# A scoring kernel's first two chunks: splits moved ahead of copies, two blocks taken part by part, one store halved

## The chip, the cores and the metric

The kernel runs on one core of one Trainium2 chip. The metric is the device time of one execution in microseconds, lower is better. The engines are named as in the profile: PE is TensorE (matmuls, PEld its weight loads), DVE is VectorE, ACT is ScalarE, POOL is GpSimd, and SP is the queue of SyncE that issues most DMAs.

## What is computed

1024 sequences of 50 item numbers, a table of 100001 rows of 128 floats, and one output of 1024 x 100001 floats (409.6 MB):

```
emb = emb_table.at[0].set(0.0)
e = emb[seq]                                  # 1024 x 50 x 128
prefix = jnp.cumsum(e, axis=1)
uF = prefix / jnp.minimum(t_idx, lengths)     # running mean
y = (uF - mean) * rsqrt(var + BN_EPS) * gamma + beta      # over the batch
v = v + (x - v) / 2; spike = v >= 1; v = v - spike        # 50 steps, one neuron per feature
uF_out = spikes.mean(axis=0)                  # 1024 x 128
scores = uF_out @ emb.T                       # 1024 x 100001
```

## The kernel before

It has two phases. The first (to about 510 us) gathers rows for the 50 steps and counts the spikes of every sequence and feature. The counts end as eight weight tiles of 128 x 128, one for each *block* `n` of 128 sequences: `countA` for block 0, `countB` for blocks 1 to 4, `countC` for blocks 5 to 7. The change is in the second phase, which multiplies them with the whole table and stores 409.6 MB.

**Parts and chunks.** The table is cut into 98 *parts* `q` of 1024 rows (`HALF`). A chunk `c` holds as many parts as `WIDTHS` says: four chunks of 2, four of 3, thirteen of 6. Parts, blocks and chunks are counted from 0 here; the words "third store" and "parts three and four" of the change's title count from one and mean block 2 of chunk 0 and parts 2 and 3.

**Split of a part** (`prepare`, lines 148 to 153). PE turns the part by eight transposes into a PSUM tile `pt` (L136); ACT casts it to a high half `hi` (L152); DVE subtracts `hi` from it, which leaves `lo` (L153). Such a pair takes one place from the list `free`. A product of one block and one part (`product`, L160) is four matmuls: `hi` and `lo` for each of two banks of 512 columns.

**Blocks of a chunk** (loop from line 499). For each block, for each part of the chunk: four matmuls into a PSUM tile `po`, then one copy with a factor 1/50 into the output tile `o`, on DVE (L512) or ACT (L514) in turns of a counter `turn`. The `ps` ring of four PSUM buffers holds both `po` and `pt` tiles in the order in which the code asks for them. After a block's parts one DMA on SP stores it (`store`, L169). In chunk 0, block 0 is done before the loop, and block 1 is stored in two halves. Output tiles of chunks 0 to 3 come from four buffers `o0` to `o3`, so a block's first copy waits until the store of four blocks earlier has landed: block 7 of chunk 0 for block 3, block 0 of chunk 1 for block 4 of chunk 0, and so on.

**When the next split comes** (`ready`, L486). In chunks 0 to 3 the places for pairs are few. Chunk 0 has none over until its own parts are done with, so parts 2 and 3 are split in block 7 of chunk 0: after the copy of part 0, `free.append(split.pop(q))` gives its place to part 2 and `ready()` splits that; after the copy of part 1 the same for part 3. Part 4 is split after block 2 of chunk 1.

The schedule is written by hand: each engine runs its instructions in the order in which the code issues them, so a copy that waits for a landing holds up whatever stands behind it on its engine.

Of the kernel before, what the change touches and what calls it, by code (L numbers as in the profile page):

```python
# [12 lines left out]
F32 = mybir.dt.float32  # L13
# [7 lines left out]
P = 128  # L21
BN_EPS = 1e-5
V_TH = 1.0
HALF = 1024
KQ = HALF // P
BANK = 512
# [13 lines left out]
def rec_kernel(  # L40
# [9 lines left out]
    nc = tc.nc  # L50
    B, T = seq.shape
    N, D = table.shape
    NB = B // P
# [29 lines left out]
    split = {}  # L83

    free = []
# [4 lines left out]
    def size(q):  # L90
        return min(HALF, N - q * HALF)
# [4 lines left out]
    def group(g):  # L96
        at = g if g < AHEAD else AHEAD - 2 + g % 2
        r = rowp.tile([P, GROUP, HALF], F32, tag=f"rows{at}", name=f"rows_{g}")
        for k in range(GROUP):
            rows[g * GROUP + SHIFT + k if g else k + ASIDE * (k >= TWICE)] = r[:, k, :]  # L100
        return r

    def fetch(r, k, q, n):

        engine = nc.sync if q < held else nc.scalar
        n = min(n, parts - q)
        whole = n - (size(q + n - 1) < HALF)
        if whole:
            engine.dma_start(
                out=r[:, k : k + whole, :],  # L110
                in_=table[q * HALF : (q + whole) * HALF, :].rearrange("(q p k) d -> p q (k d)", p=P, k=KQ),
            )
        if whole < n:
            full, rest = divmod(size(parts - 1), KQ)
            c1 = (parts - 1) * HALF
            r = r[:, k + whole, :]
            if rest:
                at = full - full % 32
                nc.vector.memset(r[at : at + 32, :], 0.0)
                engine.dma_start(  # L120
                    out=r[full : full + 1, : rest * D],
                    in_=table[c1 + full * KQ : N, :].rearrange("(o k) d -> o (k d)", o=1),
                )
            if full:
                engine.dma_start(
                    out=r[:full, :],
                    in_=table[c1 : c1 + full * KQ, :].rearrange("(p k) d -> p (k d)", k=KQ),
                )
# [19 lines left out]
    def prepare(q, pt):  # L148
        turned(q, pt)
        split[q] = hi, lo = free.pop(0)  # L150
        vp, vh, vl = views(q, pt, hi, lo)
        nc.scalar.copy(vh, vp)  # L152
        nc.vector.tensor_tensor(vl, vp, vh.bitcast(F32), ALU.subtract)  # L153
# [3 lines left out]
    def product(po, q, n, k0, kw):  # L157
        kw += kw % 2
        for j, part in enumerate(split[q]):
            nc.tensor.matmul(  # L160
                po[:, :kw],
                lhsT=counts[n],
                rhs=part[:, k0 : k0 + kw],
                start=j == 0,
                stop=j == 1,
            )

    def store(n, c0, o):
        nc.sync.dma_start(out=outs[n, :, c0 : c0 + o.shape[1]], in_=o)  # L169


    with ExitStack() as ph:
# [144 lines left out]
        for t in range(T):  # L317
# [42 lines left out]
            q = sp.tile([P, 1], F32, tag="q", name=f"q_{t}")  # L360
# [20 lines left out]
            if not last:  # L381
# [16 lines left out]
                if t in (T - 8, T - 6):  # L398
                    q = (t - T + 8) // 2
# [49 lines left out]
    psum = ctx.enter_context(  # L449
        tc.tile_pool(name="psum", bufs=4, space=bass.MemoryType.PSUM, reuse_waits="tile")  # L450
    )
    opening = ExitStack()
    turn = 1
    blocks = 0
    q0 = 0
# [4 lines left out]
    def places(at):  # L460
        t = rowp.tile([P, GROUP, HALF], F32R, tag=f"rows{at}", name=f"pairs_{at}")
        free.extend((t[:, k, :], t[:, k + 1, :]) for k in range(0, GROUP, 2))

    for c, W in enumerate(WIDTHS):

        if c in (0, NARROW, MIDDLE):
            opening.close()
            if c == NARROW:
                assert third in free
                free.remove(third)  # L470
                beside.close()
            where = opening if c < MIDDLE else ctx
            op = where.enter_context(tc.tile_pool(name="o", bufs=1, reuse_waits="tile"))
            if c == 0:
                turns = [(op, f"o{k}", 2) for k in range(4)]
            elif c == NARROW:
                turns = [(op, f"o{k}", 3) for k in (2, 0, 1)]
            else:
                fourth = op.tile([P, 4, HALF], F32R, tag="pairs", name="pairs")
                free.extend((fourth[:, k, :], fourth[:, k + 1, :]) for k in (0, 2))  # L480
                turns = [(rowp, "rows2", 6), (op, "o", 6), (rowp, "rows3", 6)]
            blocks = 0
        q1 = q0 + W
        q2 = q1 + (WIDTHS[c + 1] if c + 1 < len(WIDTHS) else 0)

        def ready():  # L486
            nonlocal to_split, third
            if to_split < q2 + FURTHER.get(c, 0) and free:
                prepare(to_split, psum.tile([P, HALF], F32, tag="ps", name=f"pt_{to_split}"))
                to_split += 1  # L490

                if to_split == SHIFT:
                    t = asidep.tile([P, ASIDE, HALF], F32R, tag="aside", name="third")
                    third = (t[:, 0, :], t[:, 1, :])
                    free.append(third)
                if to_split in (GROUP + SHIFT, 2 * GROUP + SHIFT):
                    places(to_split // GROUP - 1)

        for n in range(NB):
            if c == 0 and n == 0:  # L500
                continue
            pool, tag, most = turns[blocks % len(turns)]
            blocks += 1
            o = pool.tile([P, most * HALF], F32, tag=tag, name=f"o_{c}_{n}")
            for q in range(q0, q1):
                h0 = (q - q0) * HALF
                hw = size(q)
                po = psum.tile([P, HALF], F32, tag="ps", name=f"po_{n}_{q}")
                for k0 in range(0, hw, BANK):
                    product(po[:, k0 : k0 + BANK], q, n, k0, min(BANK, hw - k0))  # L510
                if turn % 2 == 0:
                    nc.vector.tensor_scalar_mul(o[:, h0 : h0 + hw], po[:, :hw], 1.0 / T)  # L512
                else:
                    nc.scalar.mul(o[:, h0 : h0 + hw], po[:, :hw], 1.0 / T)  # L514
                turn += 1
                if c == 0 and n == 1:
                    store(n, q * HALF, o[:, h0 : h0 + hw])
                if n == NB - 1:
                    free.append(split.pop(q))
                    ready()  # L520
            if c or n > 1:
                store(n, q0 * HALF, o[:, : min(N, q1 * HALF) - q0 * HALF])
            if {0: 4, MIDDLE: 0}.get(c, 2) <= n < NB - 1:
                ready()

            if n in (1, 4) and c >= MIDDLE and to_fetch < parts:
                g, k = divmod(to_fetch - SHIFT, GROUP)
                if k or to_split >= (g - 1) * GROUP + SHIFT:
                    if k == 0:
                        r = group(g)  # L530
                    fetch(r, k, to_fetch, GROUP // 2)
                    to_fetch += GROUP // 2
        assert to_split >= q2
        q0 = q1
# [19 lines left out]
```

## Time and profile before

| what | value |
|---|---|
| time, median of 4 runs | 1574.34 us (1573.22 to 1574.96) |
| the profiled execution | 1573.87 us, span 1572.0 us |
| PE busy, share of the span | 1128.1 us, 72% |
| DVE busy | 949.5 us, 60% |
| ACT busy | 672.9 us, 43% |
| POOL busy | 380.5 us, 24% |
| DMA | 488.12 MB, mean 311 GB/s |
| mean granted PE clock | 0.949 |
| stores of scores, 1 MB each | 30, median 6.9 us from issue to landing |
| stores of scores, 3 MB each | 96, median 19.7 us |

The span is the time from the first to the last instruction of the program; the time of the execution is longer by what lies around it. Busy time is summed over both phases, so a share says little about either. The profile's second part shows the span in 40 slices, its fourth the chain of work that ended last, and its fifth the costliest groups of instructions with the idle time before each and what ended it; windows, timelines and single tiles were asked for beside it.

### The profile page before, as it was taken

The page shows a single profiled execution, that of the slowest core. Times are in us where ns is not written, and L with a number is a line of the kernel's source. Part 1 is how long each engine was busy: PE and PEld are TensorE (multiplying, and loading weights), DVE is VectorE, ACT ScalarE, POOL GpSimd, SP SyncE. Part 2 cuts the span into 40 slices and gives each one's busy share as a digit, 9 for nine tenths or more (in the row PEclk, how much of TensorE's full clock was granted, in tenths as well). Part 3 has the DMA queues.
Part 4 walks back from the last instruction along what each step waited for, and adds up shares of the span by engine and source line. Part 5 has one row for each costly group of instructions (what it writes and reads, how often), then busy time and mean ns, then how long its engine had stood idle before and what let it go on. Part 6 is the DMA issues. An engine that isn't in the chain of part 4 may idle for free.

```text
span 1572.0 us, 12254 instructions
## 1 busy us (share of the span) xinstructions
PE 1128.1 (72%) x4464; PEld 800.1 (51%) x4464; DVE 949.5 (60%) x1127; ACT 672.9 (43%) x697; POOL 380.5 (24%) x406
## 2 busy tenths in 40 slices
PE   4544444444445998899888888888888878887884
PEld 2211111111123776677666666666666666666663
DVE  5777777777778666666555554555555545555552
ACT  2333333333334545545444444444444444444442
POOL 7777777777776000000000000000000000000000
PEclk9999999999995999999999999998999999899998
DMA  9722222222121899999999999999999999999998
GB/s 344 267 52 54 52 54 52 53 53 53 52 79 47 354 413 415 422 413 399 429 430 428 422 427 426 423 400 433 425 415 423 414 426 427 420 425 426 427 389 354
DMA packets 51313, 488.12 MB, mean 311 GB/s; under 512 B 10079, under 2 KB 10336, under 8 KB 30004
## 3 DMA queue, kind: packets, MB, share of 16 engines
q1 hardware_dynamic: 30752, 430.86, 65.2%
q0 software_dynamic: 12800, 26.24, 6.2%
q10 hardware_dynamic: 7700, 30.23, 4.7%
q8 instruction: 35, 0.57, 0.1%
q14 instruction: 26, 0.21, 0.0%
HBM read 77.69 MB, written 409.60 MB: 310 GB/s over the span
## 4 chain that ended last, share of the span: by engine, by line
DMA 46%; POOL 19%; PE 16%; issue 9%; DVE 4%; ACT 4%; ACTq 0%; POOLq 0%; SPq 0%; DVEq 0%
DMA scores<-o 42%; POOL e L207 19%; PE po L160 15%; DMA e<-in_L_rec_emb_table,idx 4%; DVE o L512 3%; ACT o L514 3%; DVE pairs L153 1%; PE pt L136 1%; ACT pairs L152 0%; PE pre L324 0%; ACT hi L152 0%; DVE lo L153 0%; PE warm L310 0%; DMA idx<-in_r_seq 0%; ACTq L514 0%
## 5 line engine op out<-in xcount | busy, mean ns | idle before, releaser
L512 DVE TENSOR_SCALAR o<-po 128x1024 f32<-128x1024 f32 (+1 forms) x391 | 467.5, 1214 | 327.3 <-DMA scores<-o 184.5
L514 ACT ACTIVATE o<-po 128x1024 f32<-128x1024 f32 x391 | 391.7, 1025 | 504.0 <-DMA scores<-o 358.9
L207 POOL DMA_INDIRECT e<-in_L_rec_emb_table,idx x400 | 379.8, 950 | 123.9 <-issue 115.8
L324 PE MATMUL pre<-ident,e 128*128 128x128 f32 x400 | 180.6, 464 | 226.2 <-DMA e<-in_L_rec_emb_table,idx 224.7
L160 PE MATMUL po<-pairs,countB 128*128 128x512 f32 (+1 forms) x1120 | 292.1, 407 | 59.8 <-ACT o L514 59.8
L160 PE MATMUL po<-pairs,countC 128*128 128x512 f32 (+1 forms) x840 | 239.3, 432 | 60.3 <-ACT o L514 53.5
L160 PEld LDWEIGHTS po<-pairs,countB 128*128 128x128 f32 x1120 | 210.9, 193 | 120.9 <-ACT o L514 78.9
L324 PEld LDWEIGHTS pre<-ident,e 128*128 128x128 f32 x400 | 73.7, 185 | 336.2 <-DMA e<-in_L_rec_emb_table,idx 335.6
L160 PEld LDWEIGHTS po<-pairs,countC 128*128 128x128 f32 x840 | 167.6, 207 | 112.4 <-ACT o L514 65.3
L153 DVE TENSOR_TENSOR pairs<-pt,pairs 128x1024 fp32r<-128x1024 f32 x70 | 85.2, 1218 | 93.9 <-ACT pairs L152 93.8
L335 DVE SCALAR_TENSOR_TENSOR uF<-rlen,pre 128x512 f32<-128x512 f32 x100 | 68.3, 683 | 109.9 <-PE pre L324 109.9
L136 PE MATMUL pt<-ident,rows 128*128 128x128 f32 (+1 forms) x768 | 104.7, 281 | 9.9 <-issue 4.9
L346 ACT ACTIVATE r<-mv,eps 128x1 f32<-128x1 f32 x50 | 14.8, 295 | 222.0 <-DVE mv L342 222.0
L136 PEld LDWEIGHTS pt<-ident,rows 128*128 128x128 f32 (+1 forms) x768 | 94.2, 147 | 27.2 <-issue 11.1
L160 PE MATMUL po<-hi,countB 128*128 128x512 f32 x208 | 86.5, 416 | 13.2 <-ACT o L514 12.9
L282 PE MATMUL pre<-zT,ls 128*128 128x512 f32 x100 | 78.1, 783 | 22.8 <-DVE uF L335 18.9
L152 ACT CAST pairs<-pt 128x1024 fp32r<-128x1024 f32 x70 | 70.1, 1013 | 40.1 <-PE pt L136 40.1
L160 PE MATMUL po<-lo,countB 128*128 128x512 f32 x208 | 84.1, 404 | 0.0
L294 ACT ACTIVATE d<-v,less 128x1024 bf16<-128x1024 f32 x49 | 54.5, 1113 | 65.4 <-DVE v L379 62.2
L160 PE MATMUL po<-hi,countC 128*128 128x512 f32 x156 | 66.1, 424 | 13.6 <-ACT o L514 12.4
L376 ACT ACTIVATE v<-uF,hgb,a 128x1024 f32<-128x1024 f32 x49 | 59.2, 1208 | 30.6 <-DVE a L372 30.5
L336 DVE BATCH_NORM_STATS2 bs<-uF 128x6 f32<-128x512 f32 x100 | 69.4, 694 | 3.5
(88 smaller groups left out, 852.7 us busy)
## 6 DMA issues: line engine op xcount, KB each, us to landing
scores<-o SPq DMA_DIRECT2D x96, 3072.0 KB, 19.7
scores<-o SPq DMA_DIRECT2D x32, 1536.0 KB, 8.9
scores<-o SPq DMA_DIRECT2D x30, 1024.0 KB, 6.9
rows<-in_L_rec_emb_table ACTq DMA_DIRECT2D x19, 1536.0 KB, 29.4
scores<-o SPq DMA_DIRECT2D x8, 2896.5 KB, 17.2
rows<-in_L_rec_emb_table SPq DMA_DIRECT2D x5, 3072.0 KB, 35.2
e<-in_L_rec_emb_table,idx POOLq DMA_INDIRECT x400, 2.5
rows<-in_L_rec_emb_table SPq DMA_DIRECT2D x2, 1024.0 KB
```

Of the source, the lines that this page charges most:

```text
L136: nc.tensor.transpose(pt[:, k0 : k0 + pw], r[:pw, k0 : k0 + D], ident[:pw, :pw])
L152: nc.scalar.copy(vh, vp)
L153: nc.vector.tensor_tensor(vl, vp, vh.bitcast(F32), ALU.subtract)
L160: nc.tensor.matmul(po[:, :kw], lhsT=counts[n], rhs=part[:, k0 : k0 + kw], start=j == 0, stop=j == 1,)
L207: nc.gpsimd.indirect_dma_start(out=es[t][:, n * P : (n + 1) * P], out_offset=None, in_=table, in_offset=bass.IndirectOffsetOnAxis(ap=idx[: ...
L282: nc.tensor.matmul(pre[h], lhsT=l, rhs=zT[:, h * BANK : (h + 1) * BANK], start=t == 0, stop=False, skip_group_check=True,)
L324: nc.tensor.matmul(pre[h][:, k : k + P], lhsT=e[:, h * BANK + k : h * BANK + k + P], rhs=ident, start=False, stop=last, is_transpose=True, ...
L335: nc.vector.scalar_tensor_tensor(uF[:, cs], rlen[:, cs], 1.0 / (t + 1), pre[h], ALU.max, ALU.mult)
L336: nc.vector.bn_stats(bs[:, h, :], uF[:, cs])
L376: nc.scalar.activation(vt, uF[:, cs], AF.Identity, bias=hgb[:, 1:2], scale=a)
L512: nc.vector.tensor_scalar_mul(o[:, h0 : h0 + hw], po[:, :hw], 1.0 / T)
L514: nc.scalar.mul(o[:, h0 : h0 + hw], po[:, :hw], 1.0 / T)
```

## The change

Only the loop over blocks in the second phase changes.

- The loops over blocks and parts become one list `blockwise` of pairs (block, part). For chunk 1 its first four entries are put part by part: (0, 2), (1, 2), (0, 3), (1, 3) instead of (0, 2), (0, 3), (1, 2), (1, 3).
- In block 7 of chunk 0 the place of a part is freed, and the next part split, ahead of the output copy instead of behind it; there `turn` stands still, so that both copies go to the same engine. In all other chunks the copy still comes first.
- Block 2 of chunk 0 is stored part by part, in two DMAs of 512 KB instead of one of 1 MB.

```
-        for n in range(NB):
-            if c == 0 and n == 0:
+        blockwise = [(n, q) for n in range(1 if c == 0 else 0, NB) for q in range(q0, q1)]
+        if c == 1:
+            blockwise[: 2 * W] = [(n, q) for q in range(q0, q1) for n in range(2)]
+        os = {}
+        for n, q in blockwise:
+            if n not in os:
+                pool, tag, most = turns[blocks % len(turns)]
+                blocks += 1
+                os[n] = pool.tile([P, most * HALF], F32, tag=tag, name=f"o_{c}_{n}")
+            o = os[n]
+            h0 = (q - q0) * HALF
+            hw = size(q)
+            po = psum.tile([P, HALF], F32, tag="ps", name=f"po_{n}_{q}")
+            for k0 in range(0, hw, BANK):
+                product(po[:, k0 : k0 + BANK], q, n, k0, min(BANK, hw - k0))
+            ending = n == NB - 1
+            if ending and c == 0:
+                free.append(split.pop(q))
+                ready()
+            if turn % 2 == 0:
+                nc.vector.tensor_scalar_mul(o[:, h0 : h0 + hw], po[:, :hw], 1.0 / T)
+            else:
+                nc.scalar.mul(o[:, h0 : h0 + hw], po[:, :hw], 1.0 / T)
+            if c or not ending:
+                turn += 1
+            if c == 0 and n in (1, 2):
+                store(n, q * HALF, o[:, h0 : h0 + hw])
+            if ending and c:
+                free.append(split.pop(q))
+                ready()
+            if q + 1 < q1:
                 continue
...
-                if c == 0 and n == 1:
-                    store(n, q * HALF, o[:, h0 : h0 + hw])
-                if n == NB - 1:
-                    free.append(split.pop(q))
-                    ready()
-            if c or n > 1:
+            if c or n > 2:
                 store(n, q0 * HALF, o[:, : min(N, q1 * HALF) - q0 * HALF])
```

More of the change, by code (lines that the diff above doesn't have):

```diff
@@ L497, in ready @@
                     places(to_split // GROUP - 1)
-        for n in range(NB):
-            if c == 0 and n == 0:
-                continue
[L502 to L515, printed above, removed]
-                if c == 0 and n == 1:
-                    store(n, q * HALF, o[:, h0 : h0 + hw])
-                if n == NB - 1:
-                    free.append(split.pop(q))
-                    ready()
-            if c or n > 1:
+        blockwise = [(n, q) for n in range(1 if c == 0 else 0, NB) for q in range(q0, q1)]
```

## The prediction, on record before the result

> **What bounds the kernel now.** I read the page first: slices of engine and DMA work, then the chain. In order, the lines are the slices of DMA, 40 of 39.3 us, and the chain by engine.
>
> ```profile
> DMA  9722222222121899999999999999999999999998
> ...
> DMA 46%; POOL 19%; PE 16%; issue 9%; DVE 4%; ACT 4%; ACTq 0%; POOLq 0%; SPq 0%; DVEq 0%
> ```
>
> From slice 14 on (512 us) the DMA engines are full and the chain runs through the stores of scores. So time after 512 us is won only where a DMA engine stands idle that could have stored. Next I cut that stretch into windows (columns: window, its length, five engines, granted clock, DMA share, GB/s).
>
> ```profile
> 517.00:519.00 2.00, 2.00 (x11) 1.65 (x10) 1.22 (x1) 1.25 (x2) 0.00 (x0) 1.00 0.86 346
> 519.00:519.50 0.50, 0.50 (x4) 0.42 (x3) 0.11 (x1) 0.50 (x1) 0.00 (x0) 1.00 0.00 0
> 519.50:520.00 0.50, 0.50 (x4) 0.42 (x3) 0.50 (x1) 0.01 (x1) 0.00 (x0) 1.00 0.81 279
> ...
> 524.00:532.00 8.00, 6.07 (x33) 4.45 (x31) 4.04 (x5) 4.05 (x5) 0.00 (x0) 1.00 1.02 421
> 532.00:532.25 0.25, 0.00 (x0) 0.00 (x0) 0.25 (x1) 0.25 (x1) 0.00 (x0) 1.00 0.48 197
> 532.25:532.75 0.50, 0.00 (x0) 0.00 (x0) 0.50 (x1) 0.50 (x1) 0.00 (x0) 1.00 0.17 66
> ...
> 535.25:536.75 1.50, 1.50 (x5) 1.20 (x4) 0.60 (x1) 0.36 (x1) 0.00 (x0) 0.56 0.09 33
> ...
> 539.25:539.50 0.25, 0.25 (x5) 0.25 (x3) 0.20 (x1) 0.20 (x1) 0.00 (x0) 1.00 0.04 0
> ```
>
> Missing DMA time, length by (1 - share): 0.28 + 0.50 + 0.10 = 0.88 us before 520; 0.13 + 0.42 + 1.37 + 0.24 = 2.16 us from 532 to 539.5; 3.0 us in all. Third, ScalarE and VectorE across the second hole:
>
> ```profile
> 525.04 1.03 ACT L514 ACTIVATE o<-po 128x1024 f32<-128x1024 f32 x1 [1.85 <-DMA scores<-o]
> 527.53 1.02 ACT L514 ACTIVATE o<-po 128x1024 f32<-128x1024 f32 x1 [1.47 <-PE po L160]
> 528.45 1.92 ACT L152 CAST hi<-pt 128x1024 fp32r<-128x1024 f32 x2
> 531.82 1.02 ACT L514 ACTIVATE o<-po 128x1024 f32<-128x1024 f32 x1 [1.45 <-PE po L160]
> ...
> 529.49 1.23 DVE L153 TENSOR_TENSOR lo<-pt,hi 128x1024 fp32r<-128x1024 f32 x1 [3.21 <-ACT hi L152]
> 530.63 1.22 DVE L512 TENSOR_SCALAR o<-po 128x1024 f32<-128x1024 f32 x1
> 531.76 1.22 DVE L153 TENSOR_TENSOR lo<-pt,hi 128x1024 fp32r<-128x1024 f32 x1
> ```
>
> The copy of (block 7, part 0) sits at 527.53 in front of both hi casts. Its product was done at 525.7; it waited for block 3's store to land (527.43) and free its buffer, and part 2's split waited behind it. TensorE then has nothing until 529.51, stutters on lo at 530.77 and 533.03, falls to half clock (0.58 and 0.56 in the windows), and chunk 1's first store leaves only at 535.92. (Parts and blocks count from 0, so the title's third store is block 2's.)
>
> Last, the stores. One store is counted by 16 landing events, one per DMA engine. Block 2's is issued at 518.87; fifteen engines are done by 522.76, one at 524.93. In that moment (519.80) that engine carries 16 KB of instructions for 1.74 us. It never idles until 536.9, while the other fifteen wait. From the chunk of 600 us on one engine is last at every store, 1.5 to 8.7 us behind the first, and paces them all: in 1492 to 1508, where the DMA share is 0.79 and 0.81, it still lands a 3 MB store every 7.43 to 7.57 us. **So the end moves by the idle time of that slow engine.** It also keeps the slower pace, 2.6 us per MB against 2.5, in the 520s, and its own packet gaps are 0.84 (518.86 to 519.70), 0.23, 1.57 and 0.24: 2.88 us, near the 3.0 of the windows.
>
> **Part by part.** From issue to first packet I take 0.83 (518.87 to 519.70, 531.91 to 532.75, 535.92 to 536.75); from a copy's end to the issue 0.07; casts and copies on ACT follow each other at 0.95; from a hi to its lo 0.04; from the first lo product to the copy 1.05 (530.77 to 531.82).
>
> *Third store in halves.* One more issue on SP (0.33 us; SP waits on copies anyway). The first half's copy ends at 517.74, so it issues at 517.81 and has packets at 518.64, before the engines run dry at 518.86. The halves take 1.28 each, to 521.42; block 3's store, issued at 520.68, brings packets at 521.51. Gain 0.84 - 0.1 = 0.74, less 0.05 for 4 KB packets (0.159 us each against 0.312 for 8 KB). Row for the fixed cost of a half: block 1's halves, issued at 515.29 and 516.73, landed 1.44 apart. The Trainium skill, "DMA: Bandwidth & Descriptors", sections on the anatomy of one DMA and on bandwidth, speaks against it: some 2.0 us fixed for each DMA, and batches of 1 MiB or more; by it the half would lose about 1.3 here. The row says that queued halves do not pay that, and I go by the row.
>
> *Splits ahead of the copies.* Nothing is added: two casts, two subtractions and sixteen transposes move in their queues. Both block 7 copies now go to ACT, since the turn stands still; it is odd before (15) and after (13), so later copies keep their engine. Walk: part 2's transposes end at 526.58 as before (TensorE runs without a gap to 528.4), hi at 526.62 to 527.63, copy at 527.57 (block 3 has landed at 527.43 - 0.7), hi of part 3 at 528.52, second copy 529.47 to 530.50, store of block 7 at 530.57 instead of 531.91. DVE: lo at 527.67 to 528.9 and 529.57 to 530.8. If the landing came later than 527.5, both splits' order would still hold, and only the store would slip.
>
> *Chunk 1's first two blocks part by part.* The PSUM ring of four frees (7,0) at 528.6, so (0,2)'s lo product starts at 528.95, and its copy at 530.4, behind ACT's second copy. (1,2) fills TensorE while part 3's lo ends. (0,3) starts at 530.55, its lo at 530.83, its copy at 531.9 to 532.93, store at 533.0 instead of 535.92. (1,2)'s copy on DVE waits for block 5's landing (532.44 - 0.7 = 531.7); behind it stands only (1,3)'s, to 534.15: store at 534.2 instead of 538.74. SP waits longer for block 0's store but nothing else is queued.
>
> *Does the slow engine stay fed?* With block 2 earlier by 0.7, its block 6 packets end at 531.76; block 7's come at 531.40, margin 0.36. Its block 7 ends at 534.33, chunk 1's first store has packets at 533.83, margin 0.5; the next has 1.9. So the three later gaps go: 0.23 + 1.57 + 0.24 = 2.04. What is late next is the engine with the instruction fetch: landings from it, 0.7 earlier, free the buffers, and the slow engine has some 2.5 us queued at each. I find no gap up to 600.
>
> Sum: 0.74 - 0.05 + 2.04 = 2.7. Bounds: 0.7 if the later gaps stay, 2.9 if all close. The profiled execution took 1573.87 (span 1572.0): 1571.2 for it, 1569.3 span. The median shown is 0.47 higher: 1574.34 - 2.7 = **1571.6**.
>
> The instruction fetch stays where it is, since TensorE's instructions keep their number. The row: block 2's store landed 6.1 us after issue, a lone one like it 4.0 (535.92), so a fetch cost one engine some 2.1. The Trainium skill, "Runtime: NRT & Kernel Launch", section on instruction fetch mechanics, calls crossing a 16 KiB boundary mostly hidden. The row says otherwise for a DMA-bound stretch; by the page nothing in the sum changes.
>
> **Rivals.** (a) *The lead of the last landing is kept* (0.27). Before, the delayed engine's lag is waited out by the others, and the next fetch (555.27) starts a second one: block 6 of chunk 1 lands last at 557.42. In the walk the first lag (524.2 + 12 stores by 2.5) ends at 554.2 and covers the second: lead 3.2, 1571.1. For it: both are on different engines as far as the packets show. Against: from 600 on the slow engine, with its 2.7, is last. (b) *The holes move* (0.12): margins of 0.36 and 0.5 are thin; if ACT's row of four is late by 2 us, or the delayed engine is the slow one, only 0.7 is gained: 1573.6. Half-clock TensorE in the 530s would do it. (c) *The ring closes; slower* (0.06): (1,2) holds a PSUM buffer until its copy gets block 5's output buffer. If that landing is late, TensorE stops at (2,3), which needs it. Block 2 of chunk 1 then slips; it has 3.1 us to spare (issue 535.55, needed by 538.7). Beyond that, each us late costs one; slower than before from 5.8 us, at 7.5 us 1576.0 and at 9 over 0.2% slower. A fetch that costs 2.1 does not reach it.
>
> **How the numbers follow.** My case has 0.55. With 0.2% (3.15 us, about what a measurement of this kernel can tell from no change) and some 0.7 us of doubt in walk and medians, it lies beyond that bound 3 times in 10, case (a) somewhat over 6 in 10, (b) never: faster 0.55 x 0.3 + 0.27 x 0.68 = 0.35. Slower: most of (c), 0.05. Same: 0.60. Range: 1570.3 (case a less 0.8) to 1574.0 (case b plus 0.4).
>
> **What would show it.** In the profile after: DMA share near 1 at 519 to 519.5 and from 532 to 539.5; hi before both copies on ACT at about 526.6; SP issues near 517.8, 530.6, 533.0 and 534.2; no half clock in the 530s; scores' stores after 600 each about 2.7 us earlier. It is wrong if the DMA holes close and the end does not move (the slow engine was not the bound), or if a new hole stands where ACT's four instructions end.

## The result and the profile after

The changed kernel takes 1572.16 us, median of 40 runs (1571.9 to 1572.46); the kernel before, in the 60 runs beside it, 1574.34 us (1572.92 to 1575.69). The ratio is 0.9986 with an interval from 0.9982 to 0.9991: 2.18 us or 0.14% shorter, which is less than the 0.2% that the prediction took as the bound of "same", and inside its range. The profiled execution took 1571.4 us (span 1569.6), 2.47 us less than that of before (span 2.4 less). Medians below are of fast runs: one execution of e8 (1622.04 us, over 1.5% above the fastest of its kernel) is left out as slow.

The page after, its slices of DMA and its chain by engine:

```profile
DMA  9712221222221999999999999999999999999998
...
DMA 46%; POOL 18%; PE 16%; issue 9%; DVE 5%; ACT 4%; ACTq 0%; POOLq 0%; SPq 0%; DVEq 0%
```

Nothing has changed in kind: the end still hangs on the stores. The windows that had the holes (window, its length, PE, PEld, DVE, ACT and POOL busy, granted clock, DMA share, GB/s):

```profile
517.00:519.00 2.00, 2.00 (x11) 1.62 (x10) 1.22 (x1) 1.23 (x2) 0.00 (x0) 1.00 0.95 377
519.00:519.50 0.50, 0.50 (x4) 0.42 (x3) 0.13 (x1) 0.49 (x1) 0.00 (x0) 1.00 1.00 401
519.50:520.00 0.50, 0.50 (x4) 0.42 (x3) 0.50 (x1) 0.00 (x0) 0.00 (x0) 1.00 0.99 393
524.00:532.00 8.00, 7.78 (x42) 6.25 (x41) 4.43 (x5) 5.94 (x7) 0.00 (x0) 1.00 1.02 423
532.00:532.25 0.25, 0.25 (x2) 0.19 (x1) 0.25 (x1) 0.25 (x1) 0.00 (x0) 1.00 1.01 426
532.25:532.75 0.50, 0.50 (x4) 0.39 (x3) 0.50 (x2) 0.50 (x1) 0.00 (x0) 1.00 0.82 344
535.25:536.75 1.50, 1.50 (x8) 1.25 (x8) 0.81 (x2) 1.24 (x2) 0.00 (x0) 1.00 1.05 431
539.25:539.50 0.25, 0.25 (x3) 0.21 (x2) 0.25 (x1) 0.25 (x1) 0.00 (x0) 1.00 1.19 492
```

Of the 3.0 us of missing DMA time some 0.2 is left: 0.10 before 519 and 0.09 at 532.25 to 532.75. The clock is whole throughout, and TensorE is busy for 7.78 of the 8 us in which it was busy for 6.07. ACT across the second hole, then DVE, then SP's issues (start, duration, group; in brackets the idle time before it and what ended it):

```profile
524.00 1.03 ACT L521 ACTIVATE o<-po 128x1024 f32<-128x1024 f32 x1 [0.83 <-DMA scores<-o]
526.60 1.01 ACT L152 CAST hi<-pt 128x1024 fp32r<-128x1024 f32 x1 [1.57 <-PE pt L136]
527.50 1.03 ACT L521 ACTIVATE o<-po 128x1024 f32<-128x1024 f32 x1
528.42 1.02 ACT L152 CAST hi<-pt 128x1024 fp32r<-128x1024 f32 x1
529.32 1.97 ACT L521 ACTIVATE o<-po 128x1024 f32<-128x1024 f32 x2
531.77 1.02 ACT L521 ACTIVATE o<-po 128x1024 f32<-128x1024 f32 x1 [0.49 <-PE po L160]
```

```profile
527.64 1.23 DVE L153 TENSOR_TENSOR lo<-pt,hi 128x1024 fp32r<-128x1024 f32 x1 [1.55 <-ACT hi L152]
529.47 1.23 DVE L153 TENSOR_TENSOR lo<-pt,hi 128x1024 fp32r<-128x1024 f32 x1 [0.61 <-ACT hi L152]
531.53 2.40 DVE L519 TENSOR_SCALAR o<-po 128x1024 f32<-128x1024 f32 x2 [0.83 <-DMA scores<-o]
```

```profile
530.40 0.33 SPq L169 DMA_DIRECT2D scores<-o  x1
532.82 0.33 SPq L169 DMA_DIRECT2D scores<-o  x1
533.95 0.33 SPq L169 DMA_DIRECT2D scores<-o  x1
```

Part 2's hi now waits for its own transposes alone (1.57 behind PE), and the copy, at 527.50 where it was at 527.53, follows it. The two lo's start 1.85 and 2.29 us earlier than before. The walk of the prediction, against these rows:

| step | predicted | after |
|---|---|---|
| hi of part 2 | 526.62 | 526.60 |
| copy of (7,0) | 527.57 | 527.50 |
| hi of part 3 | 528.52 | 528.42 |
| copy of (7,1) | 529.47 | 529.32 |
| store of block 7 of chunk 0 | 530.57 | 530.40 |
| store of block 0 of chunk 1 | 533.0 | 532.82 |
| store of block 1 of chunk 1 | 534.2 | 533.95 |
| store of block 2 of chunk 1 | 535.55 | 535.81 |

**The slow engine.** The 16 landing events of each store tell where the time went. Before, the fifteenth event, which I take for the slow engine's here, came at 522.76, 525.30, 527.88, 530.47 and 533.02 for blocks 2 to 6 of chunk 0; after, at 522.01, 524.63, 527.25, 529.87 and 532.49, and then without a gap at 535.08, 537.67 and 540.30. So it is fed through all three later holes. In the following table, the *lead* of a store is how much earlier than before its last landing comes, counted from the issue of the second phase's first store in each kernel, so that the first phase is left out.

| last landing of the store that before issued at (us) | lead of after (us) |
|---|---|
| 526.35 | 0.98 |
| 548.75 | 3.30 |
| 575.35 | 2.20 |
| 640.67 | 2.29 |
| the last one | 2.28 |

From the store of 548.75 to that of 574.21 the lead is 3.1 to 3.3: that is the rival (a), the first delayed engine covering the next one, block 6 of chunk 1 landing last at 554.07 where it was forecast at 554.2. Then the slow engine takes over as the last one, the lead falls to 2.2, and stays between 2.15 and 2.52 for the remaining 990 us, but for a single store at 1.68.

### The profile page after: what moved, and what is told of

Same layout as the page of the kernel before. It is cut to its first block, busy times and chain, and to the rows that moved or that the text cites. A ratio compares the mean times of both kernels' runs of the same rounds, so it can differ in the third digit from the quotient of the medians.

```text
span 1569.6 us, 12251 instructions
## 1 busy us (share of the span) xinstructions
PE 1125.9 (72%) x4464; PEld 796.9 (51%) x4464; DVE 948.3 (60%) x1126; ACT 674.1 (43%) x698; POOL 380.4 (24%) x406
## 4 chain that ended last, share of the span: by engine, by line
DMA 46%; POOL 18%; PE 16%; issue 9%; DVE 5%; ACT 4%; ACTq 0%; POOLq 0%; SPq 0%; DVEq 0%
DMA scores<-o 42%; POOL e L207 18%; PE po L160 15%; DMA e<-in_L_rec_emb_table,idx 4%; DVE o L519 3%; ACT o L521 3%; PE pt L136 1%; DVE pairs L153 1%; ACT pairs L152 0%; ACT hi L152 0%; PE pre L324 0%; DVE lo L153 0%; DVE uF L335 0%; DVE bs L336 0%; PE warm L310 0%
```

## The experiments

All kernels are the changed one with the edit shown, unless said. Medians stand beside those of before, run on the same chip: 1573.32 us (33 runs) for e1 to e4, 1573.27 (23 runs) for e5 to e8, 1573.47 (21 runs) for e9 to e12. Since half a microsecond is in question and before's own runs spread over 3 us, the lead in the traces says more than the medians do. It comes from one trace each; two traces of the changed kernel differ in it by 0.07 us at the end, two of before by 0.16.

**e1, the halves alone.**

```
-        if c == 1:
-            blockwise[: 2 * W] = [(n, q) for q in range(q0, q1) for n in range(2)]
...
-            if ending and c == 0:
-                free.append(split.pop(q))
-                ready()
...
-            if c or not ending:
-                turn += 1
+            turn += 1
...
-            if ending and c:
+            if ending:
```

> The kernel before with block 2 of chunk 0 stored in two halves, and nothing else. Theory (the end moves by the idle time of the slow DMA engine): its gap at 518.9 to 519.7 goes, less about 0.1 that comes back at 521.4; the later gaps (0.23, 1.57, 0.24 us) stay, since copy, cast and subtraction of block 7 still stand in the old order. Gain 0.6 to 0.8 us: 1573.6. Rival (what counts is the chain of waits through copies and splits, which the halves do not touch): 0 to 0.2 us.

1571.48 us (1571.08 to 1572.93), ratio 0.9990 (0.9981 to 0.9999): 1.84 less than before; the lead at the end is 1.90. Three of the eleven runs lie higher, at 1572.37 to 1572.93, and no trace shows why. This expectation was missed by more than a factor of two. ACT's timeline in its trace, and the windows:

```profile
526.25 1.03 ACT L516 ACTIVATE o<-po 128x1024 f32<-128x1024 f32 x1 [1.50 <-DMA scores<-o]
527.18 1.96 ACT L152 CAST hi<-pt 128x1024 fp32r<-128x1024 f32 x2
530.56 1.02 ACT L516 ACTIVATE o<-po 128x1024 f32<-128x1024 f32 x1 [1.42 <-PE po L160]
```

```profile
532.00:534.00 2.00, 2.00 (x10) 1.62 (x10) 1.23 (x1) 0.28 (x1) 0.00 (x0) 1.00 0.97 397
534.00:536.00 2.00, 2.00 (x11) 1.65 (x10) 1.23 (x1) 1.21 (x2) 0.00 (x0) 1.00 0.66 274
536.00:538.00 2.00, 2.00 (x15) 1.74 (x14) 1.23 (x1) 1.29 (x2) 0.00 (x0) 1.00 0.96 393
```

The order on ACT is that of before: the copy of (7,0), then both hi's. But that copy waits for block 3's landing, the landing comes 1.0 earlier because of the halves, and so the copy starts 1.3 earlier (1.0 from the first store on), both hi's with it, and TensorE too. The clock stays whole (a lo still stops TensorE twice, for 0.76 and 1.05 us, but the 1.13 us of before's wait for hi are gone), and counted from the first store block 7's store goes out 1.0 earlier, chunk 1's first one 1.6 and the second 2.6 earlier. One hole of some 0.7 us is left at 534 to 536. So the holes are coupled: an earlier landing closes most of the next hole by itself.

**e2, the splits alone.**

```
-        if c == 1:
-            blockwise[: 2 * W] = [(n, q) for q in range(q0, q1) for n in range(2)]
...
-            if c == 0 and n in (1, 2):
+            if c == 0 and n == 1:
...
-            if c or n > 2:
+            if c or n > 1:
```

> The kernel before with the splits of parts 2 and 3 ahead of block 7's copies (both copies on ScalarE), chunk 1 in the old order, block 2 stored whole. Theory: the gap at 519 stays; store of block 7 at about 530.6, first store of chunk 1 at about 533.2, so the later gaps of the slow engine close: gain 1.6 to 2.0 us, 1572.6. Rival (the part-by-part order is what closes them): under 1 us.

1571.89 us (1571.34 to 1572.05), ratio 0.9991 (0.9982 to 1.0000): 1.43 less than before, lead 1.80 at the end. As expected by the lead, a little less by the medians.

**e3, the order of chunk 1's first blocks alone.** The splits stay behind the copies and block 2 in one store; the reorder is all that is left of the change.

```
-            if ending and c == 0:
-                free.append(split.pop(q))
-                ready()
...
-            if c or not ending:
-                turn += 1
-            if c == 0 and n in (1, 2):
+            turn += 1
+            if c == 0 and n == 1:
...
-            if ending and c:
+            if ending:
...
-            if c or n > 2:
+            if c or n > 1:
```

> The kernel before with chunk 1's first two blocks part by part, splits behind the copies, block 2 stored whole. Theory: block 7's store stays at 531.9, chunk 1's first at about 535.2, its second at about 536; of the later gaps 0.7 to 1.0 us goes: 1573.5. Rival (the order alone closes them): 1.6 us or more.

1572.39 us (1571.75 to 1573.56), ratio 0.9996 (0.9987 to 1.0005): 0.93 less in the medians, inconclusive by the interval. The lead in its trace is 0.31 at 640 us and 0.65 at the end. Its windows:

```profile
532.00:534.00 2.00, 2.00 (x7) 1.52 (x6) 1.11 (x2) 0.71 (x1) 0.00 (x0) 0.50 0.97 397
534.00:536.00 2.00, 2.00 (x10) 1.65 (x9) 0.98 (x2) 1.02 (x1) 0.00 (x0) 0.99 0.36 147
```

TensorE has work from part to part (busy in all of both windows), but at half clock in the first of them, and the DMA engines idle for 1.3 of 2 us in the second. The reorder alone fills the wait for part 3's lo and leaves the late start: chunk 1's first store, forecast 0.7 earlier, leaves 0.02 earlier than before's, its second 1.71.

**e4, all but the halves.**

```
-            if c == 0 and n in (1, 2):
+            if c == 0 and n == 1:
...
-            if c or n > 2:
+            if c or n > 1:
```

> The changed kernel with block 2 stored whole. Theory: the gap at 519 is back, the later ones stay closed: gain 1.5 to 1.8 us against before, 1572.7, about 0.6 us behind the changed kernel, and within 0.2 us of splits alone. Rival (the three edits do not add up, since one late engine hides another): the same as the changed kernel, 1572.2.

1571.79 us (1571.60 to 1572.12), ratio 0.9991 (0.9982 to 1.0000): 1.53 less than before, lead 1.60 at the end, as expected. Taken from the whole change, the halves are worth 0.7 in lead; alone, 1.9. The three parts alone give 1.84 + 1.43 + 0.93 = 4.2 us in medians, and the whole 2.2 (on its own 60 and 40 runs): they do not add up, since each closes some of the same holes.

**e5, the turns of the copies as before.** The copy of (7,1) goes to DVE again.

```
-            if c or not ending:
-                turn += 1
+            turn += 1
```

> The changed kernel, but the turn goes on in block 7 of chunk 0, so that its second copy is VectorE's, behind part 3's subtraction. Theory: that copy starts at about 530.8 instead of 529.3, block 7's store is issued at about 532.0 instead of 530.4, the slow engine runs dry at 531.8 and gets packets at 532.8: about 0.9 us of the 2.4 is lost, 0.7 to 1.1 us behind the changed kernel, about 1572.4 where before is 1573.3. Rival (only the casts' place counts, not the copies' engine): no difference to the changed kernel.

1571.68 us (1571.33 to 1572.04), ratio 0.9992 (0.9983 to 1.0001); lead 1.76 at the end against 2.28 and 2.35 of the whole change. By the lead it loses 0.5 to 0.6; by the medians, 1.59 less than before against 2.18 and 1.93, it loses 0.3 to 0.6. The sign is as expected, the size below what was expected. The copy stands behind both lo's on DVE, so block 7's store leaves when before's did. The windows of 530 to 532, first of the changed kernel and then of e5:

```profile
530.00:532.00 2.00, 2.00 (x10) 1.59 (x9) 1.17 (x2) 1.51 (x3) 0.00 (x0) 1.00 1.04 430
```

```profile
530.00:532.00 2.00, 2.00 (x9) 1.35 (x9) 2.00 (x3) 1.00 (x2) 0.00 (x0) 1.00 0.57 234
```

DVE is full there and the DMA share is 0.57: 0.86 us of idle transfers, of which the end moves by 0.5 to 0.6. The turn that stands still is part of the gain and not a detail.

**e6, the splits ahead of the copies in every chunk.** This asks whether the holes at the ends of the later chunks, with shares of 0.87 to 0.94, can be turned into time.

```
-            if ending and c == 0:
+            if ending:
...
-            if ending and c:
-                free.append(split.pop(q))
-                ready()
```

> The changed kernel with the splits ahead of the copies in the last block of every chunk, not of chunk 0 alone. In the changed kernel the DMA share falls below 0.85 at the chunk ends near 716, 1036, 1236 and 1500 us, some 6 us of DMA time in all. Theory (the slow engine alone sets the end, and it has work there): these holes shrink and the end does not move: within 0.4 us of the changed kernel. Rival (every hole in the mean DMA share costs time): 3 to 6 us faster, 1566 to 1569.

1571.19 us (1570.94 to 1571.58), ratio 0.9987 (0.9978 to 0.9996); lead 2.37 at the end, against 2.28 and 2.35 in the two traces of the changed kernel. Two of those windows, in the changed kernel and in e6:

```profile
1024.00:1044.00 20.00, 18.52 (x68) 14.72 (x68) 12.45 (x11) 10.43 (x11) 0.00 (x0) 0.83 0.94 398
1224.00:1244.00 20.00, 16.62 (x60) 13.10 (x61) 11.31 (x10) 9.94 (x10) 0.00 (x0) 0.83 0.91 389
```

```profile
1024.00:1044.00 20.00, 17.72 (x63) 13.31 (x64) 11.53 (x10) 9.09 (x10) 0.00 (x0) 0.86 1.00 427
1224.00:1244.00 20.00, 16.55 (x64) 12.29 (x63) 10.65 (x9) 9.30 (x10) 0.00 (x0) 0.91 0.99 424
```

The holes are gone in these two (1.2 and 1.8 us by length times missing share become 0 and 0.2), and 704 to 720 goes from 0.87 to 0.92, 1488 to 1508 from 0.89 to 0.94; the end moves by 0.1 at most. So those holes are the fifteen engines waiting for the sixteenth, and cost nothing. This is the clearest sign that the mean DMA share does not set the end, and that one engine does.

**e7 and e10, relieving the slow engine.** One late store is made in two DMAs with the rows split, 120 and 8 rows in e7 and 64 and 64 in e10. By the theory, e7 takes rows from the slow engine, if that is the one left out, so that it catches up; e10 asks whether the split of the rows as such costs time. **e8** does as e7 in five stores.

```
+    def store(n, c0, o, shed=False):
+        for rows_ in (slice(0, 120), slice(120, P)) if shed else (slice(0, P),):
+            nc.sync.dma_start(out=outs[n, rows_, c0 : c0 + o.shape[1]], in_=o[rows_, :])
...
+                store(n, q0 * HALF, o[:, : min(N, q1 * HALF) - q0 * HALF], (c, n) == (len(WIDTHS) - 1, 3))
```

> The changed kernel with one store of the last chunk (block 3) issued as two DMAs, of 120 and of 8 rows, so that 15 engines carry 8 rows and one carries none, and the 8 rows go to other engines. Theory, if the engine that is left out is the slow one: it loses 7 us of work, its lag of 5.4 us at the end turns into a lead, and the end is set by the next slowest, 3.5 us earlier at most, less up to 0.9 for the extra row: 2.5 to 3.5 us faster than the changed kernel, about 1568. If another engine is left out: 0 to 1 us slower. Rival (all engines together set the end): 0 to 0.2 us slower.

> The changed kernel with five such stores, block 3 of chunks 5, 9, 13, 17 and 20. Theory, if the slow engine is the one left out: from 600 us on it falls behind by about 0.12 us with every 1.5 MB store and 0.2 with every 3 MB store, some 25 us in all if the others were not held back; the others' holes at the chunk ends (6 to 12 us) then become the limit: 5 to 10 us faster than the changed kernel, 1561 to 1566. If another engine is left out: 0 to 5 us slower. Rival (all engines together): 0 to 1 us slower.

> The changed kernel with one store of the last chunk (block 3) as two DMAs of 64 rows, for the cause of the 11 us that the split in 120 and 8 rows cost, where packets of that time took 1.6 to 1.8 us instead of 0.86. Theory: rows that go to other engines than in a store of 128 rows meet another engine's traffic on the way, so 64 rows, 4 for each engine, also slow the packets: 3 to 10 us slower than the changed kernel. Rival (it was the uneven share of 15 engines and 8 rows): 64 rows share evenly, packets at 0.86 us, within 0.5 us of the changed kernel.

e7: 1583.26 us (1583.11 to 1584.02), ratio 1.0066 (1.0053 to 1.0079), 11 to 12 us slower than the changed kernel (1572.16, and 1571.54 in e11) in place of the gain: theory and rival both missed. e8: 1607.45 us (five runs, 1595.27 to 1616.52), ratio 1.0209 (1.0167 to 1.0250), missed as widely, at some 7 us for each of five stores. e10, a single run: 1580.24 us (span 1578.5), 8.7 us above the changed kernel, within what was expected there. The windows around the split store, of the changed kernel, e7 and e10:

```profile
1528.00:1540.00 12.00, 10.18 (x46) 8.14 (x46) 5.15 (x5) 4.64 (x5) 0.00 (x0) 1.00 1.01 429
```

```profile
1528.00:1540.00 12.00, 5.91 (x26) 4.57 (x25) 3.88 (x4) 3.19 (x4) 0.00 (x0) 0.87 0.96 232
```

```profile
1528.00:1540.00 12.00, 7.95 (x33) 6.34 (x34) 4.52 (x6) 4.80 (x5) 0.00 (x0) 0.94 1.02 230
```

The DMA engines are as busy as ever (0.96 to 1.02) and move 232 and 230 GB/s instead of 429. Packets of 23 KB that take 0.87 us in the changed kernel took 1.7 us in e7 and 1.8 us in e10 from 1528 to 1540 (medians), while a quarter of them kept their time. So after a split by rows most packets run at half speed, even at 64 rows each; why, no run here shows. Whether the slow engine can be relieved in another way stays open.

**e9, before with TensorE kept warm.** To tell how much of the gain is the half clock of the 530s, part 3's eight transposes are done twice in the kernel before; the second set writes the same values again.

```
-        for k0 in range(0, HALF, P):
+        for k0 in (2 if q == 3 else 1) * list(range(0, HALF, P)):
```

> The kernel before with part 3's eight transposes done twice, into the same tile; nothing else changes, and the second pass lies in TensorE's idle time at 528.4 to 529.5. It asks whether TensorE's half clock at 533.2 to 536.6 in the profile of before is part of the price. Theory: with less idle time the clock stays whole in more runs, chunk 1's first store leaves about 0.55 us earlier (535.4) and its second about 1.6 (537.1), so 0.6 to 0.9 us of the slow engine's gaps goes: 1572.5 where before is 1573.3, and the runs lie closer together. Rival (the half clock is only a mark of the wait, the waits on copies and casts set the stores): same as before within 0.3 us.

> The kernel before, for a second trace of it: its runs lie between 1572 and 1574.8. Theory: where the run is a fast one, TensorE's clock stays whole in the 530s and the slow engine's gap at 535 to 537 is shorter by the difference; where it is near 1574, the gap is 1.4 us as in the first trace. Rival (the spread comes from the first phase or from instruction fetches): the same gaps, other start of the stores or another engine delayed.

1572.89 us (1572.23 to 1573.91), ratio 0.9997 (0.9988 to 1.0006): inconclusive as a time. In the trace chunk 1's first two stores leave 0.53 and 1.52 earlier than before's, as expected, and the lead at the end is 0.60. e12 is before itself once more (1573.6 us, span 1571.8). Windows of e9, then of e12:

```profile
532.00:534.00 2.00, 1.35 (x6) 1.13 (x7) 0.94 (x2) 0.48 (x1) 0.00 (x0) 1.00 0.90 373
534.00:536.00 2.00, 2.00 (x11) 1.64 (x10) 1.40 (x2) 1.02 (x1) 0.00 (x0) 1.00 0.57 234
```

```profile
532.00:534.00 2.00, 1.10 (x3) 0.91 (x4) 0.85 (x1) 0.72 (x1) 0.00 (x0) 0.62 0.83 340
534.00:536.00 2.00, 2.00 (x7) 1.57 (x6) 1.23 (x1) 0.00 (x0) 0.00 (x0) 0.53 0.51 209
```

Both traces of before have half clock for 3.4 us, from 533.2 and from 532.5, and both have the same gaps; eight more transposes remove it. That is worth 0.4 to 0.6 of the 2.3 us (e12's own lead over the first trace of before is 0.16), and the rest does not come from the clock. e12's run is near the median, so what differs in before's runs near 1572 stays open.

**e11, the changed kernel again**, on the chip of e9, e10 and e12.

> The changed kernel again, so that it stands on one chip beside the others: 1.5 to 2.3 us faster than before, 1571.4 where before is 1573.3, runs within 0.7 us of each other; its lead over before in landings about 2.3 us from 600 us on, as in its first profile.

1571.54 us (1571.07 to 1571.67), ratio 0.9987 (0.9978 to 0.9996), 1.93 less than before there; span 1569.3, lead 2.35. Its eleven runs lie within 0.6 us; before's on that chip spread from 1572.13 to 1574.99. What the runs of before near 1572.1 do differently, no trace caught.

## Why the prediction was right, and where it was off

*What the end follows.* Held. From 577 us on the last landings move by what the slow engine gained: e6 closes holes of the mean share and the end stays.

*Third store in halves, 0.69.* Held inside the whole change: the slow engine's landing of block 2 comes 0.70 earlier, counted from the first store, and e4 against the whole change gives 0.7 in lead. The fifteen engines had landed the first half at 520.67 and the second at 522.01, 1.34 us apart, half of a whole store's 2.5 to 2.6 and little more: no fixed cost of microseconds shows. The rule of the Trainium skill's page "DMA: Bandwidth & Descriptors" (section on the anatomy of one DMA), by which a half pays some 2.0 us for itself, would have put a loss there (the page gives the figure for DMAs issued from GpSimd; these stores are issued on SP); these rows decide against it for stores that queue.

*Splits and order, 2.04.* The walk held within 0.26 us at every step, the slow engine was fed throughout as the margins said, and the DMA share and clock in the 530s became what was to be seen.

*The sum, 2.7 where the lead at the end is 2.28, and 2.35 in e11.* This is the term that was mis-sized. The step took the slow engine's gain as kept once it had been made. But between its landings of 522.01 and 532.49 its lead over before, counted from the first store, shrank from 0.70 to 0.48: it needed 2.62 per store there against before's 2.54 to 2.59. It lost another 0.22 in the next three stores, with 2.60 each against 2.53 when before's gaps of 2.04 are taken out. By 540.30 its lead is 2.30, so the whole shortfall has arisen by then, and it is one of pace and not of a gap that stayed. The traces of e11 and e12 repeat the first half of it (2.62 against 2.56 per store). A pace of 2.6 was in the prediction; that before's is a little better was not. Why it is, in a stretch from 522 to 532 in which both kernels keep the engine fed, no run shows. The profiled execution took 1571.4 against 1571.2 forecast.

*The median, 1571.6 for 1572.16.* 2.7 was taken from a median of 1574.34 and 2.18 came. The mis-sized term is most of that. The remaining 0.1 lies within the spread of before's runs. On e11's chip the medians differ by 1.93 where the lead is 2.35; there some runs of before end near 1572.1, and why is not shown.

*Parts as separate terms.* The step that gave each edit its own holes was wrong, and the sum hid it. The prediction's lower bound, 0.7 if the later gaps stay, has no ground in the halves acting alone: they give 1.9, because an earlier landing frees the buffer that held up the copy and the hi's behind it, and TensorE's clock stays whole. The same coupling leaves rival (b), the holes moving, with less ground than its 0.12. Rival (a) ran true from the store of 548.75 for some 25 us and then gave way to the slow engine, for the reason stated against it. Rival (c), the PSUM ring, never closed: TensorE does not wait between 528.6 and 537.

## What to carry to other kernels

Where one store is counted by several engines' landings, read the landing events one by one: the mean DMA share shows holes that are only fifteen engines waiting for the sixteenth, and in this case time was won only where that one idled. Edits along one chain of buffers and landings are not to be added up; ask of each what it brings forward for the next, and try each one alone. In a queue that runs in program order, put work that another engine waits for ahead of a copy that itself waits for a landing, and look at which engine the copies then fall to (e5: 0.5 to 0.6 us).

## What was not expected of the hardware

- A store split by rows, even in two halves of 64 partitions, moved 230 GB/s where whole stores move 429, with the engines as busy as before (0.96 to 1.02): 8.7 and 11 to 12 us for one store of 2.9 MB. The split by columns in chunk 0 did nothing of the kind.
- Three gaps of TensorE of 1.13, 0.76 and 1.07 us within 4.6 us, none longer, were followed by half clock from 533.2 to 536.6 in before. The Trainium skill's page "TensorE: Matmul & The Clock Gate" (section "What's actually happening") puts the fall behind an idle window of about 3.4 us; the single gaps here are a third of that. In e3 half clock follows gaps of 0.81 and 0.76; in e1, with 0.14, 0.76 and 1.05, and in e9, with 0.29, 0.76 and 1.05, the clock stays whole. The sum of the gaps does not order these (1.57 in e3, 1.95 in e1). Where they fall does: all changes of the clock in a trace lie on one grid with steps of 3.41 us. In the step ahead of the fall TensorE is idle for 1.83 us in before, 1.71 in e12 and 1.57 in e3; in e1 and e9 a boundary of the grid (530.66 and 531.48) lies between the two long gaps, and no step has more than 1.05. By this reading, e1's whole clock is in part the luck of where its gaps fell. It is no threshold: elsewhere in these traces the clock fell after steps in which TensorE was busy for up to 0.55 of the time, and stayed whole after some with 0.44. What the gate counts is not settled.
- The mean granted clock of the profiled execution after was 0.809, and 0.943 in e11; the difference lies in the first phase, and the times differ by 0.3 us (1571.4 and 1571.07).
